# A macaron layer on one core: the weight check and its branch moved behind the float32r layers

## The chip, the cores and the metric

The kernel runs on one core of a Trainium2 chip. Its time is the device time of one execution in microseconds (us), told as the median of several runs. Span means the stretch of the profiled execution from the first to the last instruction of the program.

The engines are named as in the profile: PE is TensorE's matmul side and PEld its weight loads, DVE is VectorE, ACT is ScalarE, POOL is GpSimd and SP is SyncE, which here issues every DMA. Each engine works through its own instructions in the order in which the kernel emits them, and semaphores carry what one waits for from another.

## What is computed

A macaron layer over 16 sequences of 512 rows with 256 columns in float32: half a gated feed-forward step, attention, and half the same feed-forward step again, each added to `x`.

```python
def _L0_ffn_ref(x, w_gate, w_up, w_down):       # int32 weights, 768 hidden columns
    wg, wu, wd = (w.astype(x.dtype) * (1.0 / 127.0) for w in (w_gate, w_up, w_down))
    gate = jnp.einsum('bsd,hd->bsh', x, wg)
    up = jnp.einsum('bsd,hd->bsh', x, wu)
    return jnp.einsum('bsh,dh->bsd', jax.nn.silu(gate) * up, wd)
x = x + 0.5 * _L0_ffn_ref(_layernorm(x), w_gate, w_up, w_down)
x = x + _L0_attn_ref(_layernorm(x), ...)        # projections with bias, rope, softmax, weighted sum
x = x + 0.5 * _L0_ffn_ref(_layernorm(x), w_gate, w_up, w_down)
```

The integer weights lie within plus and minus 127 for the inputs that are timed.

## The kernel before

There are 48 stages: 16 feed-forward stages (one for each sequence `b`, stages 0 to 15), 16 attention stages (16 to 31), and 16 feed-forward stages (32 to 47). All of `x` stays in SBUF.

Float32r is a form of float32 in which a matmul runs in one pass but with fewer bits. So that nothing is lost, an activation is split into two float32r planes, `high` (the rounded value) and `low` (the rest), and each product is made twice. Integer weights up to 4096 (`EXACT`) are held by float32r without loss. The kernel checks that: it takes the largest absolute value of each part of the weights (`large`), counts the parts that are over (`over`, `count`, `flag`), loads the count into a register on every engine (`values_load`, L240), and branches (`tc.If(general == 0)`, L642) either to the layers in float32r (`layers(True, ...)`) or to the same layers in plain float32 (`layers(False, ...)`). The float32 copy isn't run for these inputs.

Ahead of the branch stands a prologue. `x[0]`, the three weights and `x[1]` to `x[3]` are loaded. PE turns over idle matmuls (`idle`). The norm of sequence 0 is measured on DVE, finished on ACT and POOL, and applied on ACT (`z`, L174). PE transposes `z`, ACT writes `high0` from the transposed tile in PSUM, and DVE writes `low0`. POOL casts the weights `wg_r` and `wu_r`, and ACT casts `wd_r`. DVE's four reductions over the weights (L213) and the count lie in between. `second.measure` takes the statistics of sequence 1.

A feed-forward stage (`ffn`) goes through six blocks `h` of 128 hidden columns. A block has eight matmuls of 512 columns into two PSUM banks, `gate` and `up` (L405: the two planes, two weights, two halves of the 256 inputs), then `act` on ACT (L413), `tr` on DVE (L415), the planes `hT_h` on ACT (L287) and `hT_l` on DVE (L292), and eight matmuls of 256 columns that add into two accumulator banks (L385, `down`). `down` is kept back by two blocks (`LAG`), so that `down(0)` of a stage stands behind the products of its block 2, and `down(5)` behind the products of block 1 of the next stage. When `down(5)` is done, DVE adds the result to `x` (`finish`, L359, twice); only then may the next stage's `down(0)` write the two accumulator banks. `gate` and `up` take turns in four PSUM banks (`ps_mm`), and `tr` in two (`ps_tr`).

Between the blocks, work for later stages is emitted by hand, by the function `beside(h)`: at `h` and at `h + 0.5`. For a later stage, `measure` takes the row statistics on DVE (L144, L146). `newton` makes the reciprocal root on POOL in 14 small instructions and `shifts` adds two (L157 to L168). `norm` applies it on ACT (L174, four instructions). `turn` transposes blocks on DVE (L332), sends them to DRAM and reads them back through SP (L317, L320). `split` makes the planes `zT_h` on ACT (L287) and `zT_l` on POOL (L292). A steady stage `i` measures stage `i+3` at 0 and 2, splits stage `i+1` at 1, turns stage `i+2` at 3, and norms stage `i+3` at 4 and 5. Stage 0 has its own list (`opening`): it norms stage 1 at 2 and 2.5, transposes it on PE at 3.5 and 4.5 (L190, copies at L497 and L500), measures stage 3 and norms stage 2 at 5, and turns stage 2 at 5.5.

An order that is emitted by hand is kept (`manual_schedule`). So an instruction that waits holds up everything behind it on its engine.

## Time and profile before

| what | value |
|---|---|
| median of 3 runs | 914.99 us (914.37 to 915.22) |
| the profiled execution | 914.53 us, span 912.7 us |
| PE busy | 902.5 us, 99% of the span |
| DVE, ACT, POOL busy | 73%, 46%, 35% of the span |
| granted TensorE clock, mean | 0.997 |
| first matmul of stage 0, of stage 1 | 13.17 us, 30.17 us |
| DMA | 103.33 MB, 113 GB/s |

A row of the groups says: the line, the engine, the operation, what it writes `<-` what it reads, the shape, the count, then busy time, mean duration of one, and the idle time before. A row of the timeline begins with the start in us from the span's start and the time from the first to the last of the instructions merged in it. In a list of one line's instructions the three numbers are the shortest, the median and the longest duration in ns. A `q` behind an engine means its sequencer. Durations of one instruction overlap the next on ACT and DVE by about 0.1 us, so the distance from start to start is less than the duration.

### The profile page before, as it was taken

What the parts mean: (1) busy time and instruction counts of PE and PEld (TensorE: products, weight loads), DVE (VectorE), ACT (ScalarE), POOL (GpSimd) and SP (SyncE); (2) the same over time, 40 slices, a digit from 0 to 9 for tenths busy, and PEclk for the clock granted to TensorE, in tenths of its full rate; (3) what the DMA queues carried; (4) which work ended last, traced back from release to release, by engine and by line L of the source; (5) the groups of instructions that cost most, each with busy time, mean ns of one, the idle gap of its engine ahead of it and who ended that gap; (6) DMA issues with size and microseconds to landing.
All of it is one profiled execution on the core that took longest, in us unless ns stands there. A gap on an engine that the chain in (4) does not pass through costs nothing.

```text
span 912.7 us, 13169 instructions
## 1 busy us (share of the span) xinstructions
PE 902.5 (99%) x4398; PEld 712.0 (78%) x4398; DVE 667.2 (73%) x1385; ACT 420.1 (46%) x715; POOL 321.2 (35%) x907
## 2 busy tenths in 40 slices
PE   8999999999999999999999999999999999999997
PEld 5899999999976666666666666666899999999996
DVE  6877777777787777777777777777777778777765
ACT  6776666666642222222222211111566676666653
POOL 3434244433432533333333333333433424343310
PEclk9999999999999999999999999999999999999999
DMA  6232423231123443443444334444422322323221
GB/s 230 106 126 76 140 93 124 84 108 55 70 70 124 131 138 116 136 132 122 128 129 138 115 116 138 139 139 138 139 93 93 115 94 94 116 93 115 94 70 50
DMA packets 54509, 103.33 MB, mean 113 GB/s; under 512 B 6176, under 2 KB 31392, under 8 KB 52384
## 3 DMA queue, kind: packets, MB, share of 16 engines
q1 hardware_dynamic: 54432, 102.39, 34.6%
q8 instruction: 37, 0.61, 0.3%
q14 instruction: 40, 0.33, 0.1%
HBM read 53.09 MB, written 49.28 MB: 112 GB/s over the span
## 4 chain that ended last, share of the span: by engine, by line
PE 97%; ACT 1%; DVE 1%; DMA 0%; issue 0%; POOL 0%; POOLq 0%
PE mm L405 36%; PE acc L385 18%; PE o_ps L587 12%; PE mm L568 12%; PE mm L517 12%; PE v_ps L548 6%; ACT z L174 0%; DMA x<-in_x_dram 0%; DVE x L359 0%; DVE tr L415 0%; ACT act L413 0%; ACT hT_h L287 0%; DVE st L144 0%; ACT L218 0%; ACT high L220 0%
## 5 line engine op out<-in xcount | busy, mean ns | idle before, releaser
L292 DVE TENSOR_TENSOR hT_l<-tr,hT_h 128x512 fp32r<-128x512 f32 (+1 forms) x193 | 129.8, 672 | 100.5 <-ACT hT_h L287 100.5
L576 ACT ACTIVATE e<-mm,top 128x512 f32<-128x512 f32 x64 | 43.9, 687 | 290.1 <-DVE top L574 290.1
L292 POOL TENSOR_TENSOR zT_l<-zT,zT_h 128x512 fp32r<-128x512 f32 x60 | 85.2, 1445 | 220.9 <-ACT zT_h L287 220.7
L287 ACT CAST hT_h<-tr 128x512 fp32r<-128x512 f32 (+1 forms) x193 | 113.1, 586 | 88.9 <-DVE tr L415 88.9
L415 DVE TENSOR_TENSOR tr<-act,mm 128x512 f32<-128x512 f32 (+1 forms) x193 | 132.8, 688 | 27.7 <-ACT act L413 14.1
L413 ACT ACTIVATE act<-mm 128x512 f32<-128x512 f32 (+1 forms) x193 | 114.8, 595 | 65.6 <-PE mm L405 64.4
L385 PEld LDWEIGHTS acc<-wd_r,hT_h 128*128 128x128 f32 x768 | 117.8, 191 | 11.4 <-ACT hT_h L287 0.7
L385 PE MATMUL acc<-wd_r,hT_h 128*128 128x256 f32 x768 | 122.6, 275 | 0.4 <-ACT hT_h L287 0.3
L385 PE MATMUL acc<-wd_r,hT_l 128*128 128x256 f32 x768 | 122.4, 275 | 0.0
L174 ACT ACTIVATE z<-x,shift,rstd 128x256 f32<-128x256 f32 x192 | 102.2, 592 | 30.3 <-POOL shift L168 30.2
L587 PE MATMUL o_ps<-v,eT 128*128 128x257 f32 x512 | 113.9, 379 | 0.0
L568 PE MATMUL mm<-krot,qrot 128*128 128x512 f32 x256 | 112.8, 592 | 0.0
L405 PE MATMUL mm<-zT_h,wg_r 128*128 128x512 f32 (+1 forms) x374 | 112.1, 381 | 0.0
L405 PE MATMUL mm<-zT_l,wg_r 128*128 128x512 f32 (+1 forms) x374 | 110.8, 378 | 0.0
L405 PE MATMUL mm<-zT_l,wu_r 128*128 128x512 f32 (+1 forms) x374 | 110.8, 378 | 0.0
L405 PE MATMUL mm<-zT_h,wu_r 128*128 128x512 f32 (+1 forms) x374 | 110.8, 378 | 0.0
L587 PEld LDWEIGHTS o_ps<-v,eT 128*128 128x128 f32 x512 | 96.9, 189 | 14.7 <-issue 0.5
L385 PEld LDWEIGHTS acc<-wd_r,hT_l 128*128 128x128 f32 x768 | 103.8, 192 | 0.0
L530 POOL TENSOR_TENSOR qrot<-r0c,r1s 128x512 f32<-128x512 f32 x16 | 20.4, 1274 | 205.7 <-DVE r1s L523 205.7
L568 PEld LDWEIGHTS mm<-krot,qrot 128*128 128x128 f32 x256 | 48.3, 190 | 54.2 <-issue 52.4
L405 PEld LDWEIGHTS mm<-zT_l,wg_r 128*128 128x128 f32 x374 | 70.5, 189 | 10.0
L405 PEld LDWEIGHTS mm<-zT_l,wu_r 128*128 128x128 f32 x374 | 70.5, 189 | 9.9
(83 smaller groups left out, 1195.8 us busy)
## 6 DMA issues: line engine op xcount, KB each, us to landing
zT_d<-blocks SPq DMA_DIRECT2D x46, 512.0 KB, 2.6
zT<-zT_d SPq DMA_DIRECT2D x184, 128.0 KB, 2.9
eT_d<-eblocks SPq DMA_DIRECT2D x16, 1024.0 KB, 3.9
eT<-eT_d SPq DMA_DIRECT2D x64, 256.0 KB, 5.0
x<-in_x_dram SPq DMA_DIRECT2D x16, 512.0 KB, 4.2
out_dram<-x SPq DMA_DIRECT2D x32, 256.0 KB, 2.1
wg_i<-in_wg_dram SPq DMA_DIRECT2D x1, 768.0 KB, 5.0
wu_i<-in_wu_dram SPq DMA_DIRECT2D x1, 768.0 KB, 6.5
```

The source lines that it names most:

```text
L174: nc.scalar.activation(self.z[:, c, :], self.x[:, c, :], AF.Identity, bias=self.shift[:, c : c + 1], scale=self.rstd[:, c : c + 1],)
L287: nc.scalar.copy(seen(high, n), source)
L292: engine.tensor_tensor(seen(low, n), source, seen(high.bitcast(F32), n), ALU.subtract)
L385: nc.tensor.matmul(accs[c // 2][:, c % 2, :], t[:, bass.ts(c % (t.shape[1] // P), P)], down_weights(h), start=h == 0 and n == 0 and c % 2 ...
L405: nc.tensor.matmul(ps, wf[w][:, k, bass.ts(h, P)], some_columns(t[:, k], columns), start=n == 0 and k == 0, stop=n == len(zT) - 1 and k == ...
L413: nc.scalar.activation(act, gate, AF.Silu, scale=WSCALE)
L415: nc.vector.tensor_tensor(hid, act, up, ALU.mult)
L517: nc.tensor.matmul(ps, w[:, k, t, :], zT[:, :, k, :], start=(k == 0), stop=(k == KD - 1))
L548: nc.tensor.matmul(ps, zT[:, a, k, :], wv_sb[:, k, :], start=(k == 0), stop=(k == KD - 1))
L568: nc.tensor.matmul(ps, q[:, t, bass.ts(a, P)], k[:, t, :], start=(t == 0), stop=(t == 1))
L576: nc.scalar.activation(e, ps, AF.Exp, bias=top, scale=1.0)
L587: nc.tensor.matmul(ps, eT[:, c, j, :], v[:, j, :], start=(j == 0), stop=(j == NC - 1))
```

## The change

- The branch ahead goes. `run(True)` emits the float32r layers at once. Behind them stand `values_load`, and a branch that runs the float32 layers over everything again if the count is above zero.
- The check goes from the prologue. The weights as loaded (`wi`) stay in buffers that attention takes later; six reductions of 768 columns (`largest`) stand in stages 3, 4 and 5, at 1.5 and 4.5; `over` stands in stage 6, `count` and `flag` in the attention stage of `b == 1`.
- Loads and casts go in parts: `x[0]` in two halves, each weight in three thirds, with `x[1]` between the fifth part and the sixth. POOL makes all casts but one, which ACT makes.
- `z` of sequence 0 is made on DVE without `shift`. The copies of `high` run in halves on ACT and DVE at once. Eleven float32r idle matmuls take the place of five in float32.
- The planes are written in another order: an inner loop over neighbouring columns of one plane, reading every second element of the source (`turned_columns`, `plane_columns`), where before the inner loop went over the two elements of a pair, which lie in two planes. That holds for `split` too.
- In stage 0, the products of blocks 0 and 1 are emitted together. Sequence 1 is measured at 1 (before: ahead of the branch), and normed at 3 and 3.5; PE transposes it at 4.5 into two banks of `ps_mm`. `measure` of stage 3 and `turn` of stage 2 go from the end of stage 0 into stage 1 (at 0 and 0.5); `turn` of stage 3 goes from 3 to 4 there, its norm from 2 to 3, and the norm of stage 4 stands whole at 5.

```diff
-    def load_x(b):
-        nc.sync.dma_start(out=xs[b], in_=x[b].rearrange("(p c) d -> p c d", c=NC))
-    order = ExitStack()
-    order.enter_context(tc.manual_schedule())
-    stage = ExitStack()
-    staged = stage.enter_context(tc.tile_pool(name="staged", bufs=1))
+    def load_x(b, tiles=slice(0, NC)):
+        nc.sync.dma_start(out=xs[b][:, tiles, :], in_=x[b].rearrange("(p c) d -> p c d", c=NC)[:, tiles, :])
     shape = {"g": [P, KD, HID], "u": [P, KD, HID], "d": [P, NH, D]}
-    wi = {w: staged.tile(shape[w], I32, name=f"w{w}_i") for w in "gud"}
-    load_x(0)
-    parts = [("g", slice(0, KD)), ("u", slice(0, KD)), ("d", slice(0, NH // 2)), ("d", slice(NH // 2, NH))]
-    for w, part in parts:
-        nc.sync.dma_start(out=wi[w][:, part, :], in_=weights[w][:, part, :])
-    for b in range(1, 4):
...
+    parts = [(w, slice(n, n + shape[w][1] // 2)) for w in "gud" for n in (0, shape[w][1] // 2)]
+    large = stat.tile([P, len(parts)], F32, name="large", bufs=1)
+    over = stat.tile([P, len(parts)], F32, name="over", bufs=1)
+    flag = stat.tile([1, 1], I32, name="flag", bufs=1)
...
-    for _ in range(5):
-        idle(S)
...
+    def turn_tile(turned, z, c):
+        for k, tr in enumerate(turned):
             tile_c = tr.rearrange("p (a c j) -> p a c j", a=NQ, j=Q)[:, :, c, :]
             nc.tensor.transpose(tile_c, z[:, c, bass.ts(k, P)], ident)
...
+    def turned_columns(tr, tiles):
+        some = slice(tiles.start * Q, tiles.stop * Q)
+        return tr.rearrange("p (a n) -> p a n", a=NQ)[:, :, some].rearrange("p a (m e) -> p e a m", e=2)
+    def plane_columns(t, k, tiles):
+        some = slice(tiles.start * Q // 2, tiles.stop * Q // 2)
+        return t[:, k].rearrange("p e (a m) -> p e a m", a=NQ)[:, :, :, some]
...
-    first = Norm(0, staged)
-    first.measure(range(NC))
-    first.root()
-    first.shifts()
-    first.norm(range(NC))
...
-    for n, (w, part) in enumerate(parts):
-        nc.vector.tensor_reduce(
-            large[:, n : n + 1], wi[w][:, part, :], AX.XY, ALU.max, apply_absolute_value=True
-        )
...
-    second = Norm(1, None, "1")
-    second.measure(range(NC))
-    order.close()
-    general = nc.values_load(flag, min_val=0, max_val=len(parts) * P)
-    stage.close()
...
+            if not exact:
+                return
...
-                sources = [ready[i][:, :, k, :].rearrange("p a (f e) -> p a f e", e=2) for k in range(KD)]
-                seen = lambda t, k: t[:, k].rearrange("p e (a f) -> p a f e", a=NQ)
+                sources = [ready[i][:, :, k, :].rearrange("p a (f e) -> p e a f", e=2) for k in range(KD)]
+                seen = lambda t, k: plane_columns(t, k, slice(0, NC))
...
+                pairs = [[ps_mm.tile([P, nt * P], F32, name="mm", tag="mm") for _ in "gu"] for _ in hs]
+                turns = [(w, k) for w in range(2) for k in range(KD)]
+                if len(hs) > 1:
+                    turns.sort(key=lambda turn: turn[1])
...
+                if h not in found:
+                    found.update(products([0, 1] if exact and i == 0 and h == 0 else [h]))
+                hid = hidden(*found.pop(h))
...
-            first = i == 2 * B
-            split_at = {1: 4, 2 * B: 4, 2 * B + 1: 3}.get(i, 1)
+            first = i == 2 * B or exact and i == 1
+            split_at = {2 * B: 4, 2 * B + 1: 3}.get(i, 1)
+            if exact:
+                split_at = {1: 4, 2: 3}.get(i, split_at)
...
+                if exact and i == 1 and h == 0.5:
+                    turn(2)
+                if exact and i in (3, 4, 5) and h in (1.5, 4.5):
+                    largest(2 * (i - 3) + (h > 3))
+                if exact and i == 6 and h == 0.5:
+                    nc.vector.tensor_scalar(over, large, EXACT, None, ALU.is_gt)
...
+        def largest(n):
+            w, part = parts[n]
+            nc.vector.tensor_reduce(
+                large[:, n : n + 1], wi[w][:, part, :], AX.XY, ALU.max, apply_absolute_value=True
+            )
+        def planes_on_tensor(i, engines, beside=lambda c: None):
+            pool, name = (ps_tr, "tr") if i == 0 else (ps_mm, "mm")
+            turned = [pool.tile([P, S], F32, name=name) for _ in range(KD)]
+            ready[i] = high, low = [work.tile(PLANE, F32R, name=f"zT_{n}", tag=f"zT_{n}") for n in "hl"]
+            for c in range(NC):
+                beside(c)
+                turn_tile(turned, norms[i].z, c)
+            for tiles in [slice(0, 2), slice(2, 4)] if i == 0 else [slice(0, NC)]:
+                for k, copy in enumerate(engines):
+                    copy(plane_columns(high, k, tiles), turned_columns(turned[k], tiles))
+            for k in range(KD):
+                nc.vector.tensor_tensor(
+                    low[:, k],
+                    turned[k].rearrange("p (m e) -> p e m", e=2),
+                    high[:, k].bitcast(F32),
+                    ALU.subtract,
+                )
+        def prologue():
+            def load_w(w, n):
+                part = (slice(0, KD), bass.ts(n, D)) if w in "gu" else (slice(2 * n, 2 * n + 2), slice(0, D))
+                nc.sync.dma_start(out=wi[w][:, part[0], part[1]], in_=weights[w][:, part[0], part[1]])
+            def cast(copy, w, n):
+                if w == "d":
+                    copy(wr[w][:, n], wi[w][:, 2 * n : 2 * n + 2, :].rearrange("p n (f e) -> p e n f", e=2))
+                else:
+                    copy(wr[w][:, :, bass.ts(n, D)], wi[w][:, :, bass.ts(n, D)])
+            nc.gpsimd.memset(eps, EPS)
+            still = work.tile([P, S], F32R, name="still", tag="rope", bufs=6)
+            nc.gpsimd.memset(still.bitcast(F32), 0.0)
+            make_identity(nc, ident)
+            nc.gpsimd.memset(one, 1.0)
+            nc.scalar.activation(root, eps, AF.Sqrt)
+            def idle(columns):
+                ps = ps_mm.tile([P, S], F32, name="mm")
+                nc.tensor.matmul(ps[:, :columns], still[:, :P], still[:, :columns], start=True, stop=True)
+            load_x(0, slice(0, 2))
+            load_x(0, slice(2, 4))
+            for w, n in (("g", 0), ("u", 0), ("g", 1), ("u", 1), ("d", 0)):
+                load_w(w, n)
+            load_x(1)
+            for w, n in (("d", 1), ("g", 2), ("u", 2), ("d", 2)):
+                load_w(w, n)
+            for b in (2, 3):
+                load_x(b)
+            for _ in range(11):
+                idle(S)
+            measure(0, (0, 1))
+            measure(0, (2, 3))
+            first = norms[0]
+            first.root()
+            first.z = work.tile([P, NC, D], F32, name="z", bufs=1)
+            for c in range(NC):
+                nc.vector.tensor_scalar(
+                    first.z[:, c, :],
+                    first.x[:, c, :],
+                    first.mv[:, c, 0:1],
+                    first.rstd[:, c : c + 1],
+                    ALU.subtract,
+                    ALU.mult,
+                )
+            cast(nc.gpsimd.tensor_copy, "g", 0)
+            cast(nc.scalar.copy, "u", 0)
+            planes_on_tensor(0, (nc.scalar.copy, nc.vector.tensor_copy), lambda c: idle(P))
+            for _ in range(2):
+                idle(S // 2)
+            nc.scalar.activation(root, eps, AF.Silu)
+            for w, n in (("g", 1), ("u", 1), ("d", 0), ("d", 1), ("g", 2), ("u", 2)):
+                cast(nc.gpsimd.tensor_copy, w, n)
+            return cast
...
         def opening(h):
-            if h == 0:
+            if h == 1:
+                measure(1, range(NC))
+                newton(1)
+            elif h == 2:
                 load(0)
-            elif h == 2:
+                cast(nc.gpsimd.tensor_copy, "d", 2)
+            elif h == 3:
                 measure(2, range(NC))
                 newton(2)
                 norm(1, (0, 1))
-            elif h == 2.5:
+            elif h == 3.5:
                 norm(1, (2, 3))
-            elif h in (3.5, 4.5):
-                k = int(h) - 3
-                tr = turned_on_tensor(norms[1].z, k)
-                if k == 0 and exact:
-                    ready[1] = [work.tile(PLANE, F32R, name=f"zT_{n}", tag=f"zT_{n}") for n in "hl"]
-                elif k == 0:
-                    ready[1] = [work.tile(PLANE, F32, name="zT_w", tag="zT_h")]
-                nc.scalar.copy(chunk(ready[1][0], k), columns(tr))
-                if exact:
-                    high, low = ready[1]
-                    nc.vector.tensor_tensor(chunk(low, k), columns(tr), chunk(high.bitcast(F32), k), ALU.subtract)
+            elif h == 4.5:
+                planes_on_tensor(1, (nc.scalar.copy, nc.scalar.copy))
             elif h == 5:
-                measure(3, range(NC))
-                newton(3)
                 norm(2, range(NC))
-            elif h == 5.5:
-                turn(2)
...
-            ready[0] = [high0, low0]
+            wi = {
+                w: pool.tile(shape[w], I32, name=f"w{w}_i", tag=tag, bufs=bufs)
+                for w, pool, tag, bufs in (("g", work, "eT", 2), ("u", work, "eT", 2), ("d", att, "eblocks", 1))
+            }
+            cast = prologue()
...
+            if exact and b == 1:
+                count = ps_acc.tile([1, len(parts)], F32, name="acc")
+                nc.tensor.matmul(count, one, over, start=True, stop=True)
+                with nc.allow_low_precision(reason="a count of at most 6 * P"):
+                    nc.vector.tensor_reduce(flag, count, AX.X, ALU.add)
...
-    with tc.If(general == 0) as arms:
+    def run(exact):
         with tc.tile_pool(name="work", bufs=2) as work, tc.tile_pool(name="att", bufs=2) as att:
             with tc.manual_schedule():
-                layers(True, work, att)
-    with arms.Else():
-        with tc.tile_pool(name="work", bufs=2) as work, tc.tile_pool(name="att", bufs=2) as att:
-            with tc.manual_schedule():
-                layers(False, work, att)
+                layers(exact, work, att)
+    run(True)
+    general = nc.values_load(flag, min_val=0, max_val=len(parts) * P)
+    with tc.If(general > 0):
+        run(False)
```

## The prediction, made before the changed kernel was run

> **What bounds the kernel now.** I read the page first: busy shares, then the chain that ended last.
>
> ```profile
> PE 902.5 (99%) x4398; PEld 712.0 (78%) x4398; DVE 667.2 (73%) x1385; ACT 420.1 (46%) x715; POOL 321.2 (35%) x907
> ...
> PE 97%; ACT 1%; DVE 1%; DMA 0%; issue 0%; POOL 0%; POOLq 0%
> ```
>
> PE is the bound, so time is gained only where PE waits or runs slowly. The list of PE's waits names all of them:
>
> ```profile
> PE mm L121 <- POOL ident masks.py:199: 1.9, 1, 1.9
> PE mm L405 <- ACT high L220: 1.1, 1, 1.1
> PE acc L231 <- DVE over L229: 0.9, 1, 0.9
> PE acc L385 <- ACT hT_h L287: 0.3, 1, 0.3
> ```
>
> They lie ahead of stage 0, but for 0.3 us. So I went through the timeline of the front.
>
> ```profile
> 4.26 1.41 DVE L144 BATCH_NORM_STATS2 st<-x 128x6 f32<-128x256 f32 x4 [4.26 <-DMA x<-in_x_dram]
> ...
> 5.58 0.36 DVE L146 BATCH_NORM_AGGREGATE mv<-st 128x2 f32<-128x6 f32 x4
> ...
> 6.87 2.08 ACT L174 ACTIVATE z<-x,shift,rstd 128x256 f32<-128x256 f32 x4 [0.60 <-POOL shift L168]
> ...
> 12.13 0.15 DVE L234 TENSOR_REDUCE flag<-acc 1x1 int32<-1x4 f32 x1 [0.28 <-PE acc L231]
> ...
> 13.17 0.91 PE L405 MATMUL mm<-high,wg_r 128*128 128x512 f32 x2 [1.07 <-ACT high L220]
> ...
> 14.08 1.35 DVE L144 BATCH_NORM_STATS2 st<-x 128x6 f32<-128x256 f32 x4
> ...
> 15.79 0.23 POOL L157 TENSOR_SCALAR var<-mv 128x4 f32<-128x4 f32 x1 [6.11 <-DVE mv L146]
> ...
> 19.92 0.20 POOL L168 TENSOR_TENSOR shift<-shift,rstd 128x4 f32<-128x4 f32 x1
> ...
> 20.49 1.09 ACT L174 ACTIVATE z<-x,shift,rstd 128x256 f32<-128x256 f32 x2
> ```
>
> PE's first real matmul starts at 13.17. `flag` is done at 12.28 (12.13 + 0.15), so the branch holds PE for 0.86. Behind it stands the chain for sequence 1: statistics on DVE, sixteen POOL instructions from 15.79 to 20.12, norm on ACT at 20.49. Then the start of stage 1, and the subtraction on POOL that ends 0.09 before stage 2's first `low` matmul wants it:
>
> ```profile
> 30.17 0.60 PE L405 MATMUL mm<-zT_h,wg_r 128*128 128x512 f32 x2
> ...
> 44.72 2.83 POOL L292 TENSOR_TENSOR zT_l<-zT,zT_h 128x512 fp32r<-128x512 f32 x2
> ...
> 47.64 0.59 PE L405 MATMUL mm<-zT_l,wg_r 128*128 128x512 f32 x2
> ```
>
> The stretches show PE's clock. PE was busy for 1.41 of 3.41, and the next 3.41 were granted half the clock:
>
> ```profile
> 10.05:13.46 3.41, 1.41 (x10) 0.90 (x9) 3.09 (x6) 3.40 (x6) 0.00 (x0) 1.00 0.99 394
> 13.46:16.87 3.41, 3.41 (x10) 2.65 (x9) 2.35 (x10) 2.19 (x3) 0.82 (x4) 0.50 0.66 233
> ```
>
> Last, a steady stage, which starts at 93.94, and what reading the flag and branching takes; the longer of PE's branches is the one at the end, over the float32 copy:
>
> ```profile
> 98.55 2.07 ACT L287 CAST zT_h<-zT 128x512 fp32r<-128x512 f32 x2
> ...
> 99.29 1.28 DVE L359 SCALAR_TENSOR_TENSOR x<-acc,x 128x512 f32<-128x512 f32 x2
> ```
>
> ```profile
> L240 SPq TENSOR_LOAD <-flag x1: 458/458/458, 12.3 to 12.3; - x1
> ...
> L240 SPq FUSED_REGOPS  x1: 186/186/186, 12.8 to 12.8; - x1
> L240 SPq SEQ_ASSERT  x1: 28/28/28, 13.1 to 13.1; - x1
> ```
>
> ```profile
> L642 PEldq COMPARE_BRANCH  x2: 90/1726/3362, 12.9 to 906.2; - x2
> L642 SPq COMPARE_BRANCH  x2: 46/48/49, 13.1 to 908.6; - x2
> ```
>
> **The change, part by part.** As PE is in order and full, the change is worth the distance by which later stages start earlier, less what the end costs. I add up the queues of the new order with start-to-start distances from the rows: matmul of 512 columns 0.217, of 256 columns 0.11, an ACT or DVE instruction on 512 elements 0.49 and 0.61, statistics of one tile 0.33 plus 0.07, z 0.49, a POOL newton step 0.28. The same addition over the old order gives starts of stage 1 and 2 of 30.18 and 46.73; the trace has 30.17 and 46.78.
>
> *The front.* Loads run at 768 KB in about 1.95 (wg lands at 6.16, wu at 8.14), so the second half of `x[0]` still lands near 4.25. Half the statistics are done by then: 5.31 for all, where before it was 5.94. Root and reciprocal: 5.87. `z` on DVE, 4 at 0.25 (no row of this operation; 0.2 to 0.33 by the statistics rows of the same 256 columns): 6.87, where ACT ended at 8.95. Transposes and half copies: PE starts at 8.1 (7.5 to 8.8). That is 5.0 earlier, and the half-clocked stretch, worth 1.7, goes too if eleven idle matmuls keep PE busy up to there. In parts, 256 KB of weights take 0.65 to 0.75 and a cast on POOL 0.5 (1.46 for 1536 columns), so all casts but the last are over by 12.1 and cost PE nothing.
>
> *Sequence 1 sets the pace of stage 0.* `measure` for it moves behind `tr` of block 1 on DVE. The gate of block 0 is complete after eleven matmuls, at 10.7; act, `tr`, planes and the next `tr` end DVE's turn at 13.9. Statistics 1.69 (as 4.26 to 5.94): 15.6. POOL's sixteen instructions 4.33 (15.79 to 20.12): 20.1. ACT's four z, with `hT_h` of block 3 between: 22.7. Behind those z, ACT's act of block 4 waits. PE has by then only 40 products and 24 `down` matmuls, 8.7 + 2.7 from 8.1: it stands from 19.5 to 22.8 with 0.6 of transposes in it, then 0.5 for banks. Stage 1 starts at 26.15: of 6.7 gained, 4.0 are left.
>
> *Stage 1* now has `measure(3)` (1.69) and `turn(2)` (1.25) on DVE. `finish` ends late, and `down(0)` waits for its accumulators, 1.4 + 0.4; stage 2 starts at 43.6, 3.1 ahead. POOL, after newton for stage 4 (38.0 to 42.3), ends `zT_l` at 45.2, 0.5 late: the subtraction that was in time by 0.09 is so no more. Stage 3 starts at 59.8, 2.6 ahead. What else moves there: `newton(3)` on POOL (31.5 to 35.9) is over when newton for stage 4 can start; `norm(3)` on ACT, four z or 2.0, holds back `hT_h` of block 3 to 40.7, and `down(3)` comes at 41.9; `turn(2)` puts one write and four reads into SP's queue, behind the loads of `x[4]`, `x[5]`, wq and wk, which wait for nothing, and lands 7.3 after its transposes, as before (34.27 to 41.56), near 40.5, ahead of the split at 41.1.
>
> *The checks beside the layers.* Six reductions of 768 columns at 0.94 (L213). DVE is not full, but the one at 4.5 stands ahead of `tr` of block 5, and the one at 1.5 ahead of the statistics that POOL and then ACT wait for. In a steady stage `finish` ends 0.5 before PE wants the second accumulator (99.29 + 1.28 = 100.57; PE ends block 2's products at 99.18 + 1.73 and comes to it two matmuls later, at 101.1). A delay of 0.86 goes beyond that: by the queues 0.2, 0.6 and 0.6 in stages 4 to 6. So 1.4 of the 2.6 goes, and 1.2 is left. Bounds: nothing, and 2.5.
>
> *The other order of the planes.* `split` reads every second element and writes in line. The rows: 1.13 for the cast with a plane change at each element, 0.59 for `hT_h` in line; on POOL 1.44, against 1.27 for qrot in line. I take 0.61 and 1.38, since all writes are now in line, and the same for the copies from PSUM (1.09 before, 0.59 now). If casts and copies keep the old durations, the 1.2 becomes -1.4.
>
> The Trainium skill ("Advanced Engine Details and Errata", Memory Cachelines) speaks for the one and against the other: two hits on a 16-byte line of SBUF are full speed, which a step of two float32 has, but PSUM's lines have 8 bytes, so each element is on another. By that rule the copies from PSUM alone stay slow, and the sum would be 916.2 where the rows give 915.0. No row here reads PSUM in single elements.
>
> *The clock.* PE's stand between 19.5 and 22.8 can bring back the half clock, as 1.41 busy of 3.41 did. That costs up to 1.7, but part of it falls into stage 1's waits: 0 to 0.9; I take 0.4. The skill ("TensorE: Matmul & The Clock Gate", Part 1) says the window runs free, so executions would differ; its figure of 3.4 agrees with the 3.41 here, and the share that trips it no row settles.
>
> *The end.* SP's last instruction before was the out DMA, then the branch of 0.05. Now SP reads the flag behind it: 0.46 + 0.19 + 0.03 + gaps, 0.84 as at the head from 12.31 to 13.15. PE's jump of 3.36 stays, and lies under SP's. I take 0.84; 0 if the wait for the last out DMA hides it, 2 if the code behind the branch comes later. The count in attention: one matmul and one small DVE reduction, 0.2, with nothing waiting.
>
> *Sum*, on the profiled execution: 914.53 - 1.2 + 0.4 + 0.84 = 914.57. It stood 0.46 below the median, so against that 915.0. A measurement here can tell about 0.2%, 1.8 us.
>
> **The rivals.** *Most of the front is kept* (faster): sequence 1's z come in time, because DVE gets to its statistics earlier or POOL's chain is shorter than in the trace. For it: all that the front shows. Against: POOL's sixteen instructions measure 4.33 each time. Without that wait, the queues give 5.4 ahead: 914.53 - 5.4 + 0.84 + 0.46 = 910.4.
>
> *Reading in steps of two is no faster* (slower): every cast and copy keeps its old row, 0.93 from start to start for `zT_h`, 1.09 and 1.12 from PSUM. Place: ACT and DVE in stages 0 to 6, where checks and splits meet ahead of `finish`. Price: 1.4 behind, plus 0.84 and the same clock: 914.53 + 1.4 + 0.4 + 0.84 + 0.46 = 917.6. It decides from about 0.95 per copy. A worse form: POOL's subtraction. Up to 2.2 each its queue takes it; beyond, every feed-forward stage loses, some 18 us over stages 3 to 15 at 2.9. POOL took 1.44 for a worse pattern, so I give that little.
>
> *It does not do what it says:* the branch is not gone but stands at the end, and the checks are not beside the layers but on DVE's way. Both are in the sum.
>
> **How the numbers follow.** Forecast 0.50 (its own range 913.3 to 916.7); front kept 0.18; slow casts 0.28; POOL 0.04. So faster 0.18, same 0.50, slower 0.32. The range reaches from 911.5 (half of the first rival) to 918.5 (the second, with 0.5 more of clock and a later end).
>
> **What would show it.** Right: PE's first product near 8.1 at full clock; a wait of PE for z near 20 to 23; stage 1 near 26, stage 2 near 43.6; waits of `down` for `finish` in stages 1 and 4 to 6; `zT_h` near 0.6, `zT_l` below 1.45; a flag read behind the last out DMA. Wrong: stage 1 before 24, or PE waits in every steady stage.

## The result, and the profile after

| | before | after |
|---|---|---|
| median of 13 runs each | 914.54 us (914.27 to 915.33) | 916.58 us (916.22 to 917.47) |
| profiled execution, span | 914.53 us, 912.7 us | 917.27 us, 915.5 us |
| first matmul of stages 0, 1, 2, 3 | 13.17, 30.17, 46.78, 62.50 | 9.01, 28.23, 45.23, 61.29 |
| first matmul of stages 4, 5, 6, 7, 8 | 78.22, 93.94, 109.66, 125.38, 141.10 | 77.01, 93.05, 109.37, 125.75, 141.47 |
| last addition on DVE ends; from there to the span's end | 907.75; 4.95 | 908.44; 7.06 |

The ratio is 1.0022, with a 95% interval of 1.0015 to 1.003: slower by about 0.2%, at the edge of what the forecast called no change. The two rows of first matmuls tell most of it: 4.16 ahead at stage 0, 1.94 at stage 1, 1.21 at stage 3, 0.37 behind at stage 8. A steady stage is 15.72 long in both kernels. The profile tells the span to 0.1, so the figures of the end are good to 0.05; by the unrounded times the end is 4.99 before and 7.04 after. The profiled execution of the changed kernel is one of its longer ones, 0.7 above its median: the medians differ by 2.04, the profiled spans by 2.74.

The page's busy row and its row of the chain by engine:

```profile
PE 902.8 (99%) x4395; PEld 712.0 (78%) x4395; DVE 671.6 (73%) x1393; ACT 402.9 (44%) x710; POOL 314.9 (34%) x911
...
PE 89%; DVE 3%; POOL 3%; issue 2%; ACT 1%; DMA 1%; SPq 0%; DVEq 0%; POOLq 0%; ACTq 0%
```

PE is as busy as before, but its share of the chain is 89% where it was 97%: DVE and POOL now stand in the chain for several stages, not for the first microseconds alone. The waits of PE up to 150 (engine, line, who ended the wait, us in total, times, longest):

```profile
PE mm L166 <- ACT z L151: 1.4, 2, 0.8
PE mm L485 <- POOL still L477: 1.3, 1, 1.3
PE acc L322 <- ACT hT_h L224: 0.7, 1, 0.7
PE mm L345 <- POOL wu_r L473: 0.4, 1, 0.4
PE tr L166 <- DVE z L505: 0.2, 1, 0.2
```

The waits for the flag and for `high` are gone; a wait for sequence 1's `z` is new. In the timeline, with the `z` of sequence 0 (6.12), PE's start (9.01), and then the chain of sequence 1 from its statistics to stage 1:

```profile
3.72 0.75 DVE L121 BATCH_NORM_STATS2 st<-x 128x6 f32<-128x256 f32 x2 [3.72 <-DMA x<-in_x_dram]
...
6.12 1.72 DVE L505 TENSOR_SCALAR z<-x,mv,rstd 128x256 f32<-128x256 f32 x4
...
9.01 0.46 PE L345 MATMUL mm<-zT_h,wg_r 128*128 128x512 f32 x1 [0.43 <-POOL wu_r L473]
...
14.84 1.40 DVE L121 BATCH_NORM_STATS2 st<-x 128x6 f32<-128x256 f32 x4
...
16.61 0.23 POOL L134 TENSOR_SCALAR var<-mv 128x4 f32<-128x4 f32 x1 [3.58 <-DVE mv L123]
...
20.99 1.09 ACT L151 ACTIVATE z<-x,shift,rstd 128x256 f32<-128x256 f32 x2 [2.17 <-POOL shift L145]
...
24.07 0.79 PE L345 MATMUL mm<-zT_h,wg_r 128*128 128x512 f32 x1
...
28.23 0.38 PE L345 MATMUL mm<-zT_h,wg_r 128*128 128x512 f32 x1
```

The chain is the forecast's, link by link, 0.9 later. Then the two stretches around PE's stand, its wait for sequence 1's `z` (length, busy time of PE, PEld, DVE, ACT, POOL; then the granted clock):

```profile
20.19:23.60 3.41, 1.92 (x13) 1.02 (x11) 1.73 (x8) 2.61 (x6) 2.58 (x13) 1.00 0.00 0
23.60:27.01 3.41, 3.41 (x9) 2.62 (x10) 2.30 (x4) 1.98 (x4) 1.76 (x9) 0.50 0.01 2
```

PE was busy for 1.92 of 3.41, and the next 3.41 were granted half the clock: nine matmuls in them. Ahead of stage 2's first `low` matmuls POOL is late, where it was early before:

```profile
43.92 2.57 POOL L229 TENSOR_TENSOR zT_l<-zT,zT_h 128x512 fp32r<-128x512 f32 x2
...
46.54 0.19 PEld L345 LDWEIGHTS mm<-zT_l,wg_r 128*128 128x128 f32 x1 [0.47 <-POOL zT_l L229]
```

Last, the flag read and the branch (durations in ns: shortest, median, longest; first and last start):

```profile
L695 SPq TENSOR_LOAD <-flag x1: 479/479/479, 306.4 to 306.4; - x1
```

```profile
L696 SPq EVENT_SEMAPHORE  x8: 17/17/17, 912.1 to 912.7; - x8
...
L696 PEldq COMPARE_BRANCH  x1: 4142/4142/4142, 907.5 to 907.5; - x1
L696 DVEq COMPARE_BRANCH  x1: 72/72/72, 908.2 to 908.2; - x1
L696 SPq COMPARE_BRANCH  x1: 50/50/50, 908.8 to 908.8; - x1
...
L696 DVEq EVENT_SEMAPHORE  x1: 21/21/21, 911.5 to 911.5; - x1
```

SP reads the flag at 306.4, in attention, and not behind the last output transfer. What stands at the end is the branch: 0.05 to 0.07 long on SP and DVE, but SP's next instruction comes 3.25 after it (908.90 to 912.15) and DVE's 3.24 after (908.29 to 911.53). SP's closing list, the waits with which it ends the program, then stops once more for 1.37 (912.96 to 914.32). The kernel before has such a jump too, over its `Else`: its SP branches at 908.56, goes on 2.80 behind that branch, at 911.41, and doesn't stop a second time.

### The profile page after: what moved, and what is told of

It is laid out like the page before. It is cut to its first block, busy times and chain, and to the rows that moved or that the text cites. A ratio compares the mean times of both kernels' runs of the same rounds, so it can differ in the third digit from the quotient of the medians.

```text
span 915.5 us, 13176 instructions
## 1 busy us (share of the span) xinstructions
PE 902.8 (99%) x4395; PEld 712.0 (78%) x4395; DVE 671.6 (73%) x1393; ACT 402.9 (44%) x710; POOL 314.9 (34%) x911
## 4 chain that ended last, share of the span: by engine, by line
PE 89%; DVE 3%; POOL 3%; issue 2%; ACT 1%; DMA 1%; SPq 0%; DVEq 0%; POOLq 0%; ACTq 0%
PE mm L345 31%; PE acc L322 16%; PE o_ps L621 12%; PE mm L551 12%; PE mm L602 12%; PE v_ps L582 6%; DVE tr L359 1%; ACT z L151 1%; DVE st L121 1%; DVE large L438 1%; DMA wu_i<-in_wu_dram 1%; ACT hT_h L224 1%; DVE x L296 0%; POOL newton L139 0%; POOL newton L138 0%
## 5 line engine op out<-in xcount | busy, mean ns | idle before, releaser
L229 POOL TENSOR_TENSOR zT_l<-zT,zT_h 128x512 fp32r<-128x512 f32 x60 | 77.2, 1308 | 211.4 <-PE acc L322 145.9
L345 PE MATMUL mm<-zT_h,wg_r 128*128 128x512 f32 (+1 forms) x386 | 116.7, 383 | 0.4 <-POOL wu_r L473 0.4
L345 PE MATMUL mm<-zT_l,wg_r 128*128 128x512 f32 (+1 forms) x386 | 115.5, 380 | 0.1
L345 PE MATMUL mm<-zT_h,wu_r 128*128 128x512 f32 (+1 forms) x386 | 115.2, 379 | 0.0
L345 PE MATMUL mm<-zT_l,wu_r 128*128 128x512 f32 (+1 forms) x386 | 114.8, 378 | 0.0
L151 ACT ACTIVATE z<-x,shift,rstd 128x256 f32<-128x256 f32 x188 | 100.0, 590 | 26.5 <-POOL shift L145 26.4
L345 PEld LDWEIGHTS mm<-zT_l,wg_r 128*128 128x128 f32 x386 | 73.1, 190 | 10.9 <-POOL zT_l L229 0.5
L345 PEld LDWEIGHTS mm<-zT_h,wu_r 128*128 128x128 f32 x386 | 73.0, 190 | 10.6 <-POOL wu_r L473 0.4
```

The lines of the kernel that those rows point to most:

```text
L151: nc.scalar.activation(self.z[:, c, :], self.x[:, c, :], AF.Identity, bias=self.shift[:, c : c + 1], scale=self.rstd[:, c : c + 1],)
L229: engine.tensor_tensor(seen(low, n), source, seen(high.bitcast(F32), n), ALU.subtract)
L345: nc.tensor.matmul(pair[w], wf["gu"[w]][:, k, bass.ts(h, P)], some_columns(t[:, k], columns), start=n == 0 and k == 0, stop=n == len(zT) - ...
```

## The experiments

Theory: the lead of 4.16 goes to three things, the chain of sequence 1 with the half clock behind it, the reductions, and the jump over the float32 code. The rivals stand with each run. Rows with the same second median share their runs of the kernel before; the ratio is formed over the runs, so it can differ from that of the two medians in the fourth digit.

| run | median, before beside it | ratio (95%) | stages 1, 2, 8 | end |
|---|---|---|---|---|
| after | 916.58, 914.54 | 1.0022 (1.0015 to 1.003) | 28.23, 45.23, 141.47 | 7.06 |
| e1_no_checks | 915.08, 915.17 | 0.9997 (0.9988 to 1.0006) | 28.34, 45.37, 140.03 | 7.03 |
| e2_checks_at_4 | 915.34, 915.17 | 1.0001 (0.9992 to 1.001) | 28.61, 45.26, 139.95 | 6.97 |
| e3_early | 914.84, 915.17 | 1.0002 (0.9993 to 1.0011) | 24.09, 42.54, 138.92 | 7.01 |
| e4_short_arm | 912.91, 915.17 | 0.9974 (0.9964 to 0.9984) | 28.06, 45.00, 141.39 | 3.05 |
| e8_five_instructions | 912.88, 914.99 | 0.9975 (0.9966 to 0.9985) | 28.36, 45.07, 141.45 | 2.98 |
| b1_before_no_branch | 912.74, 914.99 | 0.9978 (0.9968 to 0.9988) | 29.93, 46.55, 140.87 | 3.18 |
| e6_old_order | 918.22, 914.99 | 1.0036 (1.0022 to 1.005) | 28.17, 44.87, 142.55 | 7.29 |
| e11_no_pair | 915.89, 914.89 | 1.0011 (1.0002 to 1.002) | 26.20, 43.53, 139.91 | 7.22 |
| e9_two_edits | 914.39, 914.89 | 0.9989 (0.998 to 0.9998) | 24.06, 44.17, 138.49 | 7.24 |
| e7_combined | 910.78, 914.99 | 0.9955 (0.9942 to 0.9969) | 23.81, 40.43, 134.75 | 6.88 |
| e10_last_out_on_act | 908.59, 914.89 | 0.9939 (0.9925 to 0.9952) | 23.89, 40.52, 134.84 | 4.60 |
| e12_best_no_pair | 908.63, 914.82 | 0.9929 (0.9916 to 0.9943) | 24.07, 40.47, 134.79 | 5.24 |

"Stages" are the first matmuls as in the first table, "end" is from the last addition on DVE to the end of the span, both of the profiled execution.

### The reductions: taken out, and moved

```diff
-                if exact and i in (3, 4, 5) and h in (1.5, 4.5):
-                    largest(2 * (i - 3) + (h > 3))
...
-                count = ps_acc.tile([1, len(parts)], F32, name="acc")
...
+                nc.gpsimd.memset(flag, 0)
```

> The changed kernel without the check of the weights: the six reductions, the comparison and the count are left out, and the flag is set to zero. Theory 1 (the reductions push VectorE's work for TensorE back where TensorE has no slack): the lead over the kernel before no longer falls in stages 3 to 6, stage 8 starts at 139.9 instead of 141.47, attention is another 0.3 shorter without the count, and the time is 914.7 (916.58 - 1.58 - 0.3). Rival (the reductions lie in VectorE's idle time, and the lead falls there for another reason, the split of the transposed z for instance): stage 8 stays at 141.3 to 141.5 and the time at 916.3 to 916.6.

From stage 2 to stage 8 the run takes 94.66 where the changed kernel takes 96.24: 1.58 less, the figure expected. (Stage 8 itself starts at 140.03 and not at 139.9, since stage 2 started 0.14 later.) In the changed kernel the wait lies ahead of `down(0)`; here is stage 5:

```profile
99.40 1.28 DVE L296 SCALAR_TENSOR_TENSOR x<-acc,x 128x512 f32<-128x512 f32 x2
...
100.20 0.30 PEld L322 LDWEIGHTS acc<-wd_r,hT_h 128*128 128x128 f32 x2 [0.42 <-ACT zT_h L224]
...
100.73 0.30 PEld L322 LDWEIGHTS acc<-wd_r,hT_h 128*128 128x128 f32 x2 [0.24 <-DVE x L296]
```

Both waits are for `finish` (L296): the first is put down to ACT, but `zT_h` ended at 100.03 and the first half of `x` later, at 100.08. Without the reductions stages 4 to 6 have no such wait. From stage 15 to stage 32, past the count, it takes 396.84 for 397.16: the other 0.32. So the rival falls.

```diff
-                if exact and i in (3, 4, 5) and h in (1.5, 4.5):
-                    largest(2 * (i - 3) + (h > 3))
-                if exact and i == 6 and h == 0.5:
+                if exact and 3 <= i < 9 and h == 4:
+                    largest(i - 3)
+                if exact and i == 9 and h == 0.5:
```

> The same six reductions, but one in each of stages 3 to 8, behind VectorE's work for hidden block 4, where it stands idle for about 2.0 us in a steady stage; the comparison moves to stage 9. Theory 1 (what costs is the place, two to a stage in the middle of VectorE's chain): stage 9 starts 1.6 earlier than in the changed kernel, time 915.0. Rival (each reduction costs TensorE 0.26 wherever it stands): six of them still cost 1.6, time 916.6.

From stage 2 to stage 8 it takes 94.69, as if there were no reductions; each still lasts 0.945. Theory 1 holds: the place costs, not the work. (The run changes two things at once, the place within a stage and one to a stage for two; which of them counts, it doesn't tell.) Its median lies 0.26 above that of the run without any of it; its attention takes 397.16, with the 0.32 of the count in it.

### The chain of sequence 1

```diff
                 cast(nc.gpsimd.tensor_copy, w, n)
+            measure(1, range(NC))
+            newton(1)
             return cast
...
-            if h == 1:
-                measure(1, range(NC))
-                newton(1)
-            elif h == 2:
+            if h == 2:
```

> The statistics of sequence 1 are taken at the end of the prologue, where VectorE is idle from 10.32 to 12.29, instead of behind hidden block 1 of stage 0. Theory 1 (the 2.2 us that stage 0 loses are the chain statistics, Newton steps, normalization of sequence 1, and the half clock that follows TensorE's idle time): stage 1 starts at 23.6 to 25.0 instead of 28.23, no window of half clock near 24 to 27, but part of that is lost again in stages 1 and 2, whose own z comes no earlier; at stage 8 some 1.8 are left, time 914.8 (912.5 to 915.3). Rival (stage 0 is held by the casts of the weights and the loads behind them): stage 1 starts at 27.5 or later, time 916 to 916.6.

Stage 1 starts at 24.09, 4.14 earlier, and in the profiled execution no stretch of half clock is granted before the end. So it was this chain that held stage 0, not the casts or loads. Of the gain, 2.55 is left at stage 8 (1.8 expected): stage 1 takes 18.45, for PE now waits 2.2 for `hT_h` in it.

```diff
-                    found.update(products([0, 1] if exact and i == 0 and h == 0 else [h]))
+                    found.update(products([h]))
```

> The changed kernel with hidden blocks 0 and 1 of stage 0 computed one after the other, as in the kernel before, instead of side by side. Theory 1 (stage 0 ends when the chain of sequence 1 ends, whatever TensorE's order is at its start): TensorE waits up to 0.6 for the low plane near 10, stage 1 starts at 28.0 to 28.5 and the time stays at 917.0 to 917.4 (1.0022 times 915.0). Rival (the pair keeps 0.5 or more of the lead): stage 1 at 28.7 or later, time 917.7 or more; or, the other way, the statistics come earlier behind block 1 and 0.5 is won.

The last case came, and larger than thought: the gate of block 0 is complete earlier, ACT's first `act` starts at 10.74 for 11.66, and the chain is 0.9 earlier to its end:

```profile
20.09 1.09 ACT L151 ACTIVATE z<-x,shift,rstd 128x256 f32<-128x256 f32 x2 [2.19 <-POOL shift L145]
...
23.18 0.70 PE L345 MATMUL mm<-zT_h,wg_r 128*128 128x512 f32 x2
...
26.20 0.38 PE L345 MATMUL mm<-zT_h,wg_r 128*128 128x512 f32 x1
```

From block 4's first matmul to stage 1 it is 3.02 here at full clock, and 4.16 in the changed kernel (24.07 to 28.23): the half clock cost 1.14 of the 2.03 between the two starts, the chain 0.89. Pairing the blocks, which lets PE work through the waits for `low`, lengthens the very chain that PE then waits for.

### The end

```diff
     with tc.If(general > 0):
-        run(False)
+        nc.gpsimd.memset(eps, 0.0)
```

> The branch at the end stays, but the second run in float32 behind it is left out and one memset stands in its place. Theory 1 (the longer end, 7.06 instead of 4.95 from the last addition on VectorE to the end of the span, is the jump over the long second arm: each engine has to fetch code from far off): the end falls to 3.5 to 4.3 and the time to 913.2 to 914. Rival 1 (the end waits for the last output transfer and the reading of the flag, as the prediction had it): the end stays at 6 to 7, time 916 to 916.6. Rival 2 (the closing semaphore instructions at the end of any program with a branch): the end falls by 1 or less.

The end falls to 3.05 and the time by 0.5% against the changed kernel. But the branch had moved: with so short an arm the engines take it at 317 to 328, in attention. There SP's next instruction follows its branch after 0.14. To keep it at the end, the arm was given an instruction of each engine that needs the last sequence:

```diff
     with tc.If(general > 0):
-        run(False)
+        with tc.manual_schedule():
+            again = ps_mm.tile([P, S], F32, name="mm", tag="mm")
+            nc.tensor.matmul(again[:, :D], ident, xs[B - 1][:, 0, :], start=True, stop=True)
+            nc.scalar.copy(xs[B - 1][:, 0, :], again[:, :D])
+            nc.vector.tensor_copy(xs[B - 1][:, 1, :], xs[B - 1][:, 0, :])
+            nc.gpsimd.tensor_copy(xs[B - 1][:, 2, :], xs[B - 1][:, 1, :])
+            nc.sync.dma_start(out=out[B - 1].rearrange("(p c) d -> p c d", c=NC), in_=xs[B - 1])
```

> The branch stays at the very end on every engine, but the float32 second run behind it is left out and five instructions stand in its place, one for each engine, that work on the last sequence. Theory 1 (the long end is the distance: the code behind some hundred to a thousand skipped instructions has to be fetched, while a branch over an instruction or two finds its target loaded, as the 0.13 to 0.14 us from branch to next instruction in the run with the short arm have it): from the last addition on VectorE to the end of the span 3.1 to 3.9 us, no gap over 1 us in SyncE's closing list, time 913.0 to 913.8 beside 915.17 for the kernel before. Rival (what counts is that all engines branch behind their last work, at any distance): the end stays at 5 to 7, time 915 to 917.2.

The instructions of the branch's line in this run:

```profile
L696 PEldq COMPARE_BRANCH  x1: 223/223/223, 907.5 to 907.5; - x1
...
L696 DVEq COMPARE_BRANCH  x1: 72/72/72, 908.2 to 908.2; - x1
L696 DVEq EVENT_SEMAPHORE  x1: 21/21/21, 908.5 to 908.5; - x1
L696 SPq COMPARE_BRANCH  x1: 50/50/50, 908.8 to 908.8; - x1
L696 SPq EVENT_SEMAPHORE  x1: 17/17/17, 909.0 to 909.0; - x1
```

The same branch at the same moment: DVE goes on after 0.18 instead of 3.24, SP after 0.14 instead of 3.25, PE's takes 0.22 instead of 4.14. The end is 2.98, so the long arm costs 4.1, and the flag read costs nothing that can be seen. The trace also shows code on the move. From 905 on, nine blocks go through the instruction queues of the changed kernel (queue, kind: packets, MB, share of 16 engines):

```profile
q14 instruction: 7, 0.06, 1.5%
q8 instruction: 2, 0.03, 1.5%
```

In the run with five instructions, and in the one without a branch, no block goes through them after 903. That is what the Trainium skill says of taken branches ("Runtime: NRT & Kernel Launch", Instruction fetch mechanics): a target outside the code that is loaded has to be fetched first; it gives no time for it; in the changed kernel it is 2.4 (ACT) to 3.25 (SP). Out transfers are later too: 3.96 from issue to landing in the changed kernel, 2.02 here.

```diff
-    general = nc.values_load(flag, min_val=0, max_val=len(parts) * P)
...
-    with tc.If(general == 0) as arms:
-        with tc.tile_pool(name="work", bufs=2) as work, tc.tile_pool(name="att", bufs=2) as att:
-            with tc.manual_schedule():
-                layers(True, work, att)
-    with arms.Else():
...
+    with tc.tile_pool(name="work", bufs=2) as work, tc.tile_pool(name="att", bufs=2) as att:
+        with tc.manual_schedule():
+            layers(True, work, att)
```

> The kernel before, but its first arm runs straight: the flag is not read, and the branch and the float32 arm are left out. It prices all that the removal of the branch could have brought there. Theory 1 (in stage 0 it is the statistics and normalization of sequence 1 that decide when stage 1 starts, not TensorE's start): TensorE starts at 12.2 to 12.6 instead of 13.17, stage 1 starts at 29.8 to 30.2 as before, the end from the last addition falls from 4.95 to 3.1, time 913.0 to 913.4 beside 915.17. Rival (the front's 0.8 is kept): stage 1 at 29.4, time 912.5.

PE starts 1.03 earlier and 0.24 of it reach stage 1: the front's gain is lost in the old code as well. The end falls from 4.95 to 3.18. So of the branch's price in the kernel before, which is 2.25, the larger part, some 1.8, lay at the end, where the change added to it.

The last edit, on top of the combined version below, lets ACT issue the last sequence's two output transfers:

```diff
-                nc.sync.dma_start(
+                queue = nc.scalar if b == B - 1 else nc.sync
+                queue.dma_start(
```

> The combined version with the output transfers of the last sequence issued by ScalarE instead of SyncE, so that SyncE branches over the float32 code well before the last work is done. Theory 1 (the end is set by SyncE's branch, 3.2 from it to its next instruction, and the stop of 1.3 in its closing list): both lie beside the work, and from the last addition to the end of the span 6.9 fall to 4.5 to 5.5, time 909.0 to 909.8 beside 910.78. Rival (the branches of VectorE and ScalarE, 2.4 to 3.3 behind their last work, and the stop in the closing list come after that anyway): the end stays at 6.3 to 7, time 910.2 to 910.8. Below zero too: the issue on ScalarE delays its branch, up to 0.7 slower.

```profile
L698 SPq EVENT_SEMAPHORE  x8: 17/17/17, 893.3 to 905.0; - x8
...
L698 SPq COMPARE_BRANCH  x1: 50/50/50, 890.2 to 890.2; - x1
```

SP jumps at 890.2 and pays its 3 us beside the work. Its last wait for the other engines' jumps is over at 905.0, when DVE goes on, so what is left of the end is the jump of the others. The end is 4.60 for 6.88, and the ratio 0.9939 for 0.9955. Theory 1 holds, a little beyond its range.

### The order of the planes

```diff
-                sources = [ready[i][:, :, k, :].rearrange("p a (f e) -> p e a f", e=2) for k in range(KD)]
-                seen = lambda t, k: plane_columns(t, k, slice(0, NC))
+                sources = [ready[i][:, :, k, :].rearrange("p a (f e) -> p a f e", e=2) for k in range(KD)]
+                seen = lambda t, k: t[:, k].rearrange("p e (a f) -> p a f e", a=NQ)
```

> The changed kernel with the planes of the transposed z read and written in the order of the kernel before (inner step over the two planes). Theory 1 (the casts lie off TensorE's path everywhere but in the first stages): ScalarE's zT_h goes from 0.84 back to 1.13 and GpSimd's zT_l from 1.31 to 1.44; stage 2 or 3 starts up to 0.6 later, the steady stage stays at 15.72, time 917.2 to 917.8 on this chip, where the changed kernel stands at about 917.2 (1.0022 times 915.17). Rival (the order is what keeps the lead that is left): 1 us or more is lost by stage 8, time 918.2 or more.

`zT_h` takes 1.134 again and `zT_l` 1.447. The durations are theory 1's, the loss is the rival's: 1.08 at stage 8. But it is not lost in the first stages. Stage 4 starts at 76.91, 0.10 earlier than in the changed kernel; stages 4 to 6 then lose 2.76 where the changed kernel loses 1.58, and PE waits for DVE's `finish` three times, 1.1 in all. So in `split` the new order is worth 1.1 where casts and reductions meet ahead of `finish`, and nothing that shows elsewhere. The copies out of PSUM for sequences 0 and 1 keep the new order in this run; what it is worth there was not run.

### Together

```diff
@@ steady and opening, besides the edits of the early statistics and the reductions at 4
-            first = i == 2 * B or exact and i == 1
+            first = i == 2 * B
-                split_at = {1: 4, 2: 3}.get(i, split_at)
+                split_at = {1: 4}.get(i, split_at)
-                if exact and i == 1 and h == 0.5:
-                    turn(2)
+                if exact and i == 1 and h == 2:
+                    norm(3, range(NC))
...
-            elif h == 3:
-                norm(1, (0, 1))
-            elif h == 3.5:
-                norm(1, (2, 3))
+            elif h == 3:
+                norm(1, range(NC))
...
             elif h == 5:
+                measure(3, range(NC))
+                newton(3)
                 norm(2, range(NC))
+            elif h == 5.5:
+                turn(2)
```

(`measure(2)` and `newton(2)` go from 3 to 2.)

> The changed kernel with three edits: statistics of sequence 1 at the end of the prologue; one reduction per stage at hidden block 4 in stages 3 to 8; and the preparation for sequences 2 and 3 in stages 0 and 1 at the places that the kernel before gave it. Theory 1: the gains add: stage 1 starts at 24.0, stage 8 at 136.0 (137.2 from the first two alone: 138.92 less the 1.7 that stages 4 to 6 still lost to the reductions; 1.2 more by the third), time 911.7 (917.2 less 5.5). Rival (the first stages are already limited by the split of the transposed z, and the third edit brings nothing): stage 8 at 137.2 or later, time 913.0.

Stage 1 at 23.81, stage 2 at 40.43, then 15.72 for each stage: 6.7 ahead of the changed kernel at stage 8, 1.25 more than expected. This version beats both kernels, and with the transfers on ACT by 0.6% the one before. To price the third edit it was left out:

> The run of the combined version without its third edit: statistics of sequence 1 in the prologue and one reduction per stage at hidden block 4, but the preparation for sequences 2 and 3 where the changed kernel has it (sequence 2's transposes and moves in stage 1, sequence 3 behind it, the split for stage 3 at block 3). Theory 1 (each edit brings its own gain): stage 2 starts at 42.5 as in the run with the early statistics alone, stage 8 at 137.2, time 913.0 to 913.3 beside 915.0 for the kernel before; the third edit is then worth 2.4 (137.2 less the combined version's 134.75). Rival (the third edit changes nothing and the two others gain more together): stage 8 at 134.7 to 135.5, time 910.8 to 911.5.

Stage 8 at 138.49: the third edit is worth 3.7 in these two profiles. But stage 2 came 1.63 later than in the run with the early statistics alone, whose code is the same up to there. The stretches say why; two of this run, then two of the one with the early statistics:

```profile
31.53:34.94 3.41, 1.54 (x10) 1.35 (x11) 3.41 (x9) 1.08 (x2) 2.31 (x12) 1.00 0.38 154
34.94:38.36 3.42, 3.42 (x11) 2.76 (x10) 2.67 (x8) 1.81 (x4) 1.13 (x6) 0.50 0.56 153
```

```profile
28.78:32.19 3.41, 2.45 (x15) 1.88 (x13) 3.41 (x12) 1.05 (x2) 1.31 (x7) 1.00 0.01 2
32.19:35.60 3.41, 2.15 (x13) 1.88 (x14) 3.41 (x9) 1.08 (x2) 1.89 (x10) 1.00 0.38 154
```

PE's stand is the same; the clock's windows of 3.41 fall 0.66 differently. In one run a window catches the stand whole (busy 1.54) and the next is halved; in the other the stand is shared between two windows (2.45 and 2.15), and nothing happens. The runs of this version fall into two groups, six at 914.39 to 914.92 with a mean granted clock of 0.996 and five at 912.99 to 913.28 with 0.997; the second is what theory 1 expected. So of the 3.7 about 1.3 is the halved window, and the rest is near the 2.4 of theory 1.

> The version with the three edits and the last output transfers on ScalarE, and hidden blocks 0 and 1 of stage 0 one after the other. Theory 1 (the pair did harm only by holding back the chain of sequence 1, which now starts in the prologue): without the pair TensorE waits some 0.4 to 0.6 for the low plane near 9.7 to 10.3, stage 1 starts at 23.8 to 24.5 where the paired version has 23.89, time 908.3 to 909.2. Rival (the pair delays the first activation, and with it everything behind it in stage 0, whatever the chain): stage 1 starts 0.5 or more earlier, at 23.4 or before, time 908.1 or less.

Stage 1 at 24.07, stage 2 at 40.47, and 908.63 for 908.59: with the statistics in the prologue the pair is worth nothing either way, as theory 1 had it.

## Why the prediction came out as it did

The time is 1.6 over the forecast and within its range. The forecast counted from 914.99 for the kernel before, which came at 914.54 in the result's runs, so the change is 2.0 slower where the sum had 0.04 (-1.2 + 0.4 + 0.84). It stayed in the range because the range was wide, not because the sum was right. On the profiled pair the span grew by 2.8. The 2.76 between that and the sum: 1.17 up to stage 8 (0.37 behind, where the sum had 0.8 ahead), 0.32 in attention, 1.27 at the end (2.11 for 0.84). All three lie on the slow side.

*Right: what paces stage 0, and the reductions.* PE's stand for sequence 1's `z`, the sixteen POOL instructions (16.61 to 20.95, 4.34) and stage 2's late subtraction (0.47 for 0.5) came as worked out, and moving that chain moved stage 1 by 4.14. The reductions were to cost 0.2, 0.6 and 0.6 in stages 4 to 6; they cost 0.32, 0.60 and 0.66. The first rival, that most of the front is kept, fell with the first of these.

*Mis-sized: the front.* PE starts at 9.01 for 8.1. `z` on DVE was put at 0.25 from the statistics rows; it is 0.32 from start to start, and one of the four, beside a cast on POOL, took 0.747:

```profile
L505 DVE TENSOR_SCALAR z<-x,mv,rstd x4: 408/412/747, 6.1 to 7.1; 128x256 f32<-128x256 f32 x4
```

That makes 1.72 for 1.0. The statistics end 0.2 later, too. The 0.9 passes through the chain unchanged: `z` at 20.99 for 20.1.

*Mis-sized: the clock.* The step took 0.4 out of 0 to 0.9, on the ground that part would fall into stage 1's waits. The run without the pair puts it at 1.14 where stage 1 starts. Together with the 0.9 this is the 2.08 by which stage 1 came later than 26.15. The ground was right in part: of the 2.03 between the two runs at stage 1, 1.70 is left at stage 2, and from stage 1 to stage 3 the changed kernel lost 0.6 to 0.7 less than the queues gave. That the stretch is halved is no accident of one execution: it is so in all six profiles that have both the pair and the late statistics.

*Mis-sized: the count.* 0.2 "with nothing waiting" was held to be free; it cost 0.32.

*Failed: the end.* The step said that SP's flag read stands behind the last output transfer and that SP pays 0.84 for it, while PE's jump lies beneath. SP reads the flag at 306.4, so that term was nothing. The jump was not PE's alone: the trace before has SP standing for 2.80 behind its own (908.60 to 911.41), and the step didn't see it. The kernel before ended at 4.95, without any branch it ends at 3.18, with the far branch at 7.06, with a near one at 2.98. What came on top of the old jump, in SP's order: the jump is 0.45 longer (3.25 for 2.80), eight more waits stand behind its target (0.6, from 912.15 to 912.76), and there is the second stop of 1.37; off this goes 0.4, since SP comes to its branch 0.41 behind the last addition and not 0.81. That "the code behind the branch comes later" stood as a bound, at 2; the measured 2.1 is about that bound, but the sum went by 0.84.

*The plane order.* The rival that reading in steps of two is no faster is refuted: copies out of PSUM take 0.598 on ACT and the subtraction 0.681 on DVE, for 1.09 and 1.12 before. The skill ("Advanced Engine Details and Errata", Memory Cachelines) names matmuls as what non-contiguous access in PSUM slows; the prediction read the rule on its lines onto the copies, and that would have left them slow. The measurement decides against this reading here. Reading in steps of two out of SBUF is not the full speed that the prediction took from the same page, though: `zT_h` is 0.844, not 0.61, where ACT's cast of `wu_i`, in line out of SBUF, took 0.62. In the run with the old order, where it is 1.134, PE loses by the slower casts on balance in stages 4 to 6 alone:

```profile
L224 ACT CAST zT_h<-zT x60: 647/844/913, 42.5 to 879.4; 128x512 fp32r<-128x512 f32 x60
```

*Small slips.* From `flag` (12.28) to PE's start (13.17) it is 0.89, not 0.86. The lower end of the range, 911.5, is not half of the first rival, which would be 912.7. Nothing above rests on either.

*Left open.* SP's closing list stops once more, for 1.24 to 1.62, in all eight profiles where the far jump lies behind the layers and SP is the last to take it. The times speak for a second fetch: in each of them a block of 8 KB starts in an instruction queue 0.56 to 0.85 behind SP's first instruction after the jump, and the stop ends 1.58 to 1.76 after that start. Where SP jumps alone (transfers on ACT), the jump itself ends 1.55 after the start of such a block. The kernel before has the block too (911.96), but its list is over 0.7 later. No edit tested this. A branch placed in the middle of the program, so that the float32 layers lie behind the other's end, was not tried.

## What to carry to other kernels

An earlier start on the bound engine is worth only as much as the next stage's preparation moves with it: look for the chain that releases the second stage, and start it in the first idle time of its engines. Work beside a full engine is free in one place and costs over a quarter of its length in another (1.58 for six reductions of 0.94), so place it by the queue of its own engine, block by block. A branch over unrolled code costs several microseconds on every engine that takes it behind its last work; let the engine that closes the program be finished early.

## What the runs showed of the hardware

- **A taken branch.** Over the float32 layers, in the changed kernel: 2.4 (ACT), 3.24 (DVE), 3.25 (SP) to the next instruction, and 4.14 for PE's. Over one or two instructions: 0.14 (SP), 0.18 (DVE), and 0.22 for PE's. With the far jump nine blocks go through the instruction queues after 905, with the near one none.
- **The clock window.** It lasts 3.41 and runs free of the program. Windows with PE busy for 1.41, 1.54, 1.92 and 1.98 were followed by one at half clock, such with 2.15, 2.45 and 2.80 were not. But PE's busy time alone doesn't settle it: at the end of three runs, windows with 1.48 (no checks), 1.65 (transfers on ACT) and 1.67 (combined) were followed by one at full clock. The Trainium skill ("TensorE: Matmul & The Clock Gate", Part 1) says that the window runs free, and the two runs above show it. The row of 1.48 and the one behind it:

```profile
904.31:907.72 3.41, 1.48 (x14) 1.29 (x12) 1.71 (x3) 0.34 (x1) 0.00 (x0) 1.00 0.25 90
907.72:911.14 3.42, 0.00 (x0) 0.00 (x0) 0.00 (x0) 0.00 (x0) 0.00 (x0) 1.00 0.26 88
```

- **DVE beside POOL.** In the twelve profiles with `z` on DVE, a `z` alone takes 0.40 to 0.41. In ten of them one `z` meets a cast on POOL, and takes 0.45 to 0.80: that one ends 0.14 to 0.15 after the cast, whenever the cast began. The skill ("SBUF — State Buffer", SBUF: two separate sides) has POOL and certain DVE operations share a port that one of them holds for a whole instruction; the rows agree. Whether `z` is such an operation by the skill's conditions, no row tells.
